# Transposing x and h with VectorE blocks, and applying the graph after the product, in a two-layer graph and attention kernel

## The chip, the cores and the metric

The kernel runs on one core of a Trainium2 chip. The metric is the device time of one launch in microseconds. The kernel before takes 3195.14 us, the median of 3 runs (3194.66 to 3195.42).

TensorE, VectorE, ScalarE and GpSimd appear in the profile as PE (weight loads as PEld), DVE, ACT and POOL; SP is the queue from which all DMAs of this kernel are issued.

## The reference, cut to what matters

There are 64 batches (x is 64 x 256 x 512, float32) and one graph `adj` of 256 x 256 with entries 0 and 1. Layer 0 mixes neighbours, layer 1 is attention with 8 heads under the graph as a mask. Both add their input and normalise.

```python
# layer 0
mi = x @ Wi.T                      # 256 x 512 per batch
mj = x @ Wj.T
deg = a.sum(axis=1)
out = deg[:, None] * (mi + b) + a @ mj
h = layernorm(x + out)
# layer 1
q, k, v = h @ Wq.T + bq, h @ Wk.T + bk, h @ Wv.T + bv
attn = softmax(where(adj == 0, -inf, q k^T / 8))
h2 = layernorm(h + (attn v) @ Wo.T + bo)
```

The graph can be applied before the product or after it: a @ (x @ Wj.T) is the same number as (a @ x) @ Wj.T. On this choice the change turns.

## The kernel before

The batches are worked in 32 pairs (`g`, with batches `b1` and `b2`). While the attention of pair g runs, layer 0 of pair g+1 is done in between, as work items dropped into the attention's slots. All products of layer 0, and the q, k, v and output projections, are done by a seven-product scheme for a 2 x 2 block matrix product (seven block products in place of eight), with sums of the left blocks S1 to S4 and of the right blocks T1 to T4. Everything is float32, except the graph product, where x is split into a rounded part `xhi` and a remainder `xlo` (both float32r) that are multiplied separately by the exactly representable graph.

Layer 0 before: TensorE computes, for each batch, degree times x and neighbour sums of x, already transposed (feature on the partitions), from x as the stationary operand. These are the left blocks of the seven products.

```python
def graph_product(b, c, pa, n, t, part):          # 16 of these for a batch, 384 columns each
    matmul(pa[:, t * P:(t + 3) * P], part[:, t, c * P:(c + 1) * P], graph[:, t, :], ...)

def take_input(b, c, pa):                         # 4 of these for a batch
    nc.scalar.copy(xl[b][:, c]..., pa[:, :3 * P])
    _, a12, a22, a21 = (pa[:, m * P:(m + 1) * P] for m in range(4))
    nc.vector.tensor_add(f["S1"][:, c], a21, f["A22"][:, c])      # 128 x 128 each
    nc.vector.tensor_sub(f["S3"][:, c], f["A11"][:, c], a21)
    nc.vector.tensor_sub(f["S2"][:, c], a22, f["S3"][:, c])
    nc.vector.tensor_sub(f["S4"][:, c], a12, f["S2"][:, c])

def l0_steps(b, norm=norm):
    def product(name, lname, n, first):           # 7 steps, 4 matmuls of 256 columns each
        for c in range(NC):
            matmul(banks[name], xS[b][lname][:, c, :], w0[:, n, c, :], ...)
    ...
    def step7():
        product("z", "S4", B22, False)
        add_to(place(0, 1), banks["z"])
        norm(xh[b][:, 0, :])

def h_transpose(b, t, borrow=False):              # 2 for a batch: h is needed with features on partitions
    for c in range(NC):
        transpose(pt[:, c, :], xh[b][:, t, c * P:(c + 1) * P], ident)      # TensorE, 128 x 128
    nc.scalar.copy(hT[g][:, :, i * N + t * P:i * N + (t + 1) * P], pt)

def split_x(b):                                   # for each batch
    round_x(b)                 # xhi, ScalarE
    remainder(b, nc.gpsimd)    # xlo, GpSimd
    add_bias(b)                # xh += degree * bias, GpSimd
```

The products go to a ring of 3 PSUM banks (`bank`), the scores to a ring of 2 slots of 2 banks (`score_banks`), the attention values to one bank. The weights of the four projections are streamed from device memory, 8 blocks ahead (`bring`, `next_factor`).

The slots of one pair: `work[0]` to `work[6]` hold layer 0 of the next pair.

```python
return [[item(l0_inputs, b1, 0, ...), item(l0_inputs, b1, 1)],
        p[0:3] + [item(split_x, b2)] + p[3:4],
        p[4:7] + [item(l0_inputs, b2, 0)],
        [item(l0_inputs, b2, 1, ...), q[0], q[1], item(h_transpose, b1, 1, True),
         q[2], item(h_transpose, b1, 0, True)],
        q[3:],
        [item(h_transpose, b2, 1, True)], [item(h_transpose, b2, 0, True)]]
```

Of the kernel before, what the change touches and what calls it, by code (L numbers as in the profile page):

```python
# [16 lines left out]
P = 128  # L17
# [203 lines left out]
RIGHT = (B11, T4, B21, T2, T1, T3, B22)  # L221
RIGHT_O = (B11, B21, T4, T2, T1, T3, B22)
# [3 lines left out]
def unshifted_path(ctx, tc, flag, x, adj, wiT, wjT, b0, wqT, bq, wkT, bk, wvT, bv, woT, bo, out):  # L226

# [16 lines left out]
    DH = 64  # L244
    NB = 2
# [47 lines left out]
    adj_i = p2.tile([P, NT, N], I32, tag="pe", name="adj_i")  # L293
    nc.sync.dma_start(out=adj_i, in_=adj.rearrange("(t p) j -> p t j", p=P))
# [6 lines left out]

    load_x(0)
    b_bc = p4.tile([P, D], F32, tag="u", name="b_bc")
    w0 = const.tile([P, 7, NC, H], F32, name="w0")

    for n, w, j in ((B11, wiT, 0), (T3, wiT, 1), (B22, wjT, 1), (B21, wjT, 0)):
        nc.sync.dma_start(out=w0[:, n], in_=w.rearrange("(c p) o -> p c o", p=P)[:, :, j * H:(j + 1) * H])
    nc.sync.dma_start(out=b_bc, in_=b0.to_broadcast([P, D]))
    load_x(1)

    xhi, xlo, xl, xS, hT, hS, qT, kT, vv, aoT, oS = ({} for _ in range(11))

    def round_x(b):

        xhi[b] = p1.tile([P, NT, D], F32R, tag="xhi", name="xhi")
        in_order(nc.scalar.copy(xhi[b], xh[b]))

    round_x(0)


# [12 lines left out]

    graph = const.tile([P, NT, 3 * P], F32R, name="graph")
# [3 lines left out]
    nc.vector.tensor_copy(a, adj_i)  # L338
    aT = p3.tile([P, NT, N], F32, tag="pk", name="aT")
    deg = small.tile([P, NT], F32, tag="deg", name="deg")  # L340
    nc.vector.tensor_reduce(deg, a, AX.X, ALU.add)

    def diagonal(t):
        return slice(2 * t * P, (2 * t + 1) * P)

    def edges(t):
        return slice((1 - t) * P, (3 - t) * P)

    for t in range(NT):
        nc.vector.tensor_scalar(graph[:, t, diagonal(t)], ident, deg[:, t:t + 1], None, ALU.mult)  # L350
    for t in range(NT):
        pt = bank("pt_a")[:, :N]
        for i in range(NT):
            transpose(pt[:, i * P:(i + 1) * P], a[:, i, t * P:(t + 1) * P], ident)

        nc.vector.tensor_copy(graph[:, t, edges(t)], pt)
        in_order(nc.scalar.copy(aT[:, t, :], pt))
# [3 lines left out]
    def check_graph():  # L361


        exact = p1.tile([P, NT, 3 * P], F32, tag="oS", name="exact")
        for t in range(NT):
            in_order(nc.vector.tensor_copy(exact[:, t, edges(t)], aT[:, t, :]))
            in_order(nc.vector.tensor_scalar(exact[:, t, diagonal(t)], ident, deg[:, t:t + 1], None, ALU.mult))
        in_order(nc.vector.tensor_tensor(exact, exact, graph.bitcast(F32), ALU.not_equal))
        in_order(nc.vector.tensor_reduce(inexact, exact.rearrange("p t n -> p (t n)"), AX.X, ALU.max))
        in_order(nc.vector.tensor_scalar(maskT, aT, 0.0, MASK, ALU.is_equal, ALU.mult))  # L370
# [5 lines left out]
    def remainder(b, engine):  # L376

        xlo[b] = p1.tile([P, NT, D], F32R, tag="xlo", name="xlo")
        in_order(engine.tensor_tensor(xlo[b], xh[b], xhi[b].bitcast(F32), ALU.subtract))

    def add_bias(b):
        in_order(nc.gpsimd.tensor_tensor(xh[b], xh[b], degb, ALU.add))

    def split_x(b):
        if b < B:
            round_x(b)
            remainder(b, nc.gpsimd)
            add_bias(b)
# [21 lines left out]
    def blocks_of(w):  # L410
        return w.rearrange("(h c p) (j o) -> p h c j o", h=2, p=P, j=2)

    sources = {}

    def load_raw(w, tag):
        raw = p1.tile([P, 2, 2, 2, H], F32, tag=tag, name="raw")
        nc.sync.dma_start(out=raw.rearrange("p h c j o -> p (h c) (j o)"),
                          in_=w.rearrange("(c p) o -> p c o", p=P))
        return raw

    def make_factors(w, name, raw):
# [3 lines left out]
        for n, (t, p, m) in enumerate(((t1, b12, b11), (t2, b22, t1), (t3, b22, b12), (t4, b21, t2))):  # L425
            in_order(nc.vector.tensor_sub(t, p, m))
            nc.sync.dma_start(out=kept[n], in_=t)
        src = blocks_of(w)
        sources[name] = {B11: src[:, 0, :, 0], B21: src[:, 1, :, 0], B22: src[:, 1, :, 1],
                         T1: kept[0], T2: kept[1], T3: kept[2], T4: kept[3]}  # L430

    def fold_value_bias(raw):

        pb = bank("pb")
        spread = p3.tile([P, NC, P], F32, tag="pk", name="spread")
        in_order(nc.vector.tensor_copy(spread, bv_t.unsqueeze(2).to_broadcast([P, NC, P])))
        for c in range(NC):
            h, kc = divmod(c, 2)
            matmul(pb, spread[:, c], raw[:, h, kc].rearrange("p j o -> p (j o)"),
                   start=(c == 0), stop=(c == NC - 1))  # L440
        nc.vector.tensor_add(bo_bc, pb, bo_bc)
# [49 lines left out]
    def input_tiles(b):  # L491
        xl[b] = p2.tile([P, NC, 3, P], F32, tag="xl", name="xl")
        a11, a12, a22 = (xl[b][:, :, m, :] for m in range(3))
        xS[b] = left_blocks(a11, a12, None, a22, p2.tile([P, 4, NC, P], F32, tag="xS", name="xS"))

    def graph_product(b, c, pa, n, t, part):
        matmul(pa[:, t * P:(t + 3) * P], part[:, t, c * P:(c + 1) * P], graph[:, t, :],
               start=(n == 0), stop=(n == 2 * NT - 1), skip_group_check=True)

    def take_input(b, c, pa):  # L500
        nc.scalar.copy(xl[b][:, c].rearrange("p m n -> p (m n)"), pa[:, :3 * P])
        _, a12, a22, a21 = (pa[:, m * P:(m + 1) * P] for m in range(4))
        f = xS[b]
        nc.vector.tensor_add(f["S1"][:, c], a21, f["A22"][:, c])
        nc.vector.tensor_sub(f["S3"][:, c], f["A11"][:, c], a21)
        nc.vector.tensor_sub(f["S2"][:, c], a22, f["S3"][:, c])
        nc.vector.tensor_sub(f["S4"][:, c], a12, f["S2"][:, c])

    def l0_inputs(b, half, borrow=()):


        if half == 0:
            input_tiles(b)
        for c in (2 * half, 2 * half + 1):
            pa = borrow[c % 2]("pa") if borrow else bank("pa")
            for n, (t, part) in enumerate((t, part) for t in range(NT) for part in (xhi[b], xlo[b])):
                graph_product(b, c, pa, n, t, part)
            take_input(b, c, pa)

    def first_inputs(b):  # L520

        input_tiles(b)
        pas = [score_banks("pa")[:, 0, :], score_banks("pa")[:, 0, :],
               ps_v.tile([P, 2, N], F32, tag="av", name="pa").rearrange("p r q -> p (r q)"), bank("pa")]
        f = xS[b]
        for k, part in enumerate((xhi[b], xlo[b])):
            for c in reversed(range(NC)):
                for t in range(NT):
                    graph_product(b, c, pas[c], k * NT + t, t, part)
                if k == 1:  # L530
                    in_order(nc.scalar.copy(xl[b][:, c].rearrange("p m n -> p (m n)"), pas[c][:, :3 * P]))  # L531

        def add(name, c, x, y, sign):
            in_order(nc.vector.tensor_tensor(f[name][:, c], x, y, ALU.add if sign > 0 else ALU.subtract))  # L534

        def sums(name):
            for c in reversed(range(NC)):
                _, a12, a22, a21 = (pas[c][:, m * P:(m + 1) * P] for m in range(4))
                if name == "S2":
                    add("S3", c, f["A11"][:, c], a21, -1)  # L540
                    add("S2", c, a22, f["S3"][:, c], -1)
                elif name == "S1":
                    add("S1", c, a21, f["A22"][:, c], 1)
                else:
                    add("S4", c, a12, f["S2"][:, c], -1)

        return sums

    def l0_steps(b, norm=norm):
        banks = {}  # L550

        def product(name, lname, n, first):
            if first:
                banks[name] = bank("po")[:, :H]
            for c in range(NC):
                matmul(banks[name], xS[b][lname][:, c, :], w0[:, n, c, :], start=(first and c == 0),
                                 stop=(c == NC - 1), skip_group_check=True)

        def place(t, j):
            return xh[b][:, t, j * H:(j + 1) * H]  # L560

        def add_to(dst, src, order=anywhere):
            order(nc.vector.tensor_add(dst, src, dst))  # L563

        def step1():
            product("x", "A11", B11, True)
            u1 = p2.tile([P, H], F32, tag="lu", name="u1")
            nc.scalar.copy(u1, banks["x"])

            rest = xh[b].rearrange("p t (j o) -> p (t j) o", j=2)[:, 1:]  # L570
            nc.gpsimd.tensor_tensor(rest, rest, u1.unsqueeze(1).to_broadcast([P, 3, H]), ALU.add)  # L571

        def step2():
# [515 lines left out]
```

## Time and profile before

| engine | busy us | share of the span | instructions |
|---|---|---|---|
| PE | 3172.0 | 99% | 17398 |
| PEld | 2621.1 | 82% | 17398 |
| DVE | 1845.7 | 58% | 3848 |
| POOL | 1501.8 | 47% | 1190 |
| ACT | 1109.4 | 35% | 2146 |

The DMA queues move 340.88 MB, at a mean of 107 GB/s. How to read it: "busy" is the time in which an engine had at least one instruction under way. A matmul's record runs from its start to its modelled end, and matmuls overlap, so the mean duration of one record is longer than what it costs in a stream; the cost in a stream is read from the timeline, as the distance of one start to the next. A float32 matmul leaves two records, a float32r matmul and a transpose one.

### The profile page before, as it was taken

The numbers are of one execution on the slowest core, as the hardware profiler recorded it, in microseconds if no ns is written. First come the engines' busy times: TensorE is split into PE (matmuls) and PEld (weight loads), VectorE is DVE, ScalarE is ACT, GpSimd is POOL, SyncE is SP. The second block draws the span as 40 slices with busy tenths as digits, with TensorE's granted clock in tenths as the row PEclk, the third lists the DMA queues.
The fourth block names the chain that finished last, engine by engine and source line by source line (L and its number), as shares of the span: only waits on it lengthen the run. The fifth ranks groups of instructions, "written<-read, shape, count | busy, mean of one in ns | idle before, by whom it ended". The sixth has DMA issues, their size and how long they took to land. (4 is left out here: it accounts for less than half of the span.)

```text
span 3195.0 us, 48126 instructions
## 1 busy us (share of the span) xinstructions
PE 3172.0 (99%) x17398; PEld 2621.1 (82%) x17398; DVE 1845.7 (58%) x3848; ACT 1109.4 (35%) x2146; POOL 1501.8 (47%) x1190
## 2 busy tenths in 40 slices
PE   8999999999999999999999999999999999999998
PEld 6888888888888888888888888888888888888885
DVE  7555556555565555665556555556555565555664
ACT  2333333343333333333333333333343333333333
POOL 2454444544445544445444454444544445544443
PEclk9999999999999999999999999999999999999999
DMA  7234432344322444323443233432344322344222
GB/s 254 68 104 119 123 112 67 96 121 124 119 72 88 116 122 123 86 79 108 126 122 95 75 106 119 124 111 67 96 121 124 116 74 88 116 122 122 82 68 92
DMA packets 257166, 340.88 MB, mean 107 GB/s; under 512 B 29856, under 2 KB 154272, under 8 KB 256928
## 3 DMA queue, kind: packets, MB, share of 16 engines
q1 hardware_dynamic: 256928, 337.76, 35.6%
q8 instruction: 142, 2.33, 0.3%
q14 instruction: 96, 0.79, 0.1%
HBM read 274.73 MB, written 37.75 MB: 98 GB/s over the span
## 5 line engine op out<-in xcount | busy, mean ns | idle before, releaser
L469 POOL TENSOR_TENSOR rstd<-ve,mhalf 128x1 f32<-128x1 f32 x256 | 140.4, 553 | 790.4 <-DVE below L467 790.4
L287 PE MATMUL po<-w,xS 128*128 128x256 f32 x2048 | 466.3, 381 | 2.5 <-DVE xS L534 2.5
L287 PE MATMUL st<-hS,factor 128*128 128x256 f32 x2048 | 454.4, 380 | 2.0 <-DVE u L670 2.0
L797 POOL TENSOR_TENSOR pk<-pe 128x512 f32<-128x512 f32 x256 | 322.8, 1276 | 276.4 <-ACT pe L794 276.4
L287 PEld LDWEIGHTS po<-w,xS 128*128 128x128 f32 x2048 | 386.3, 190 | 64.7 <-DVE rden L867 10.3
L287 PEld LDWEIGHTS st<-hS,factor 128*128 128x128 f32 x2048 | 390.2, 191 | 55.7 <-DVE u L670 2.4
L794 ACT ACTIVATE pe<-pe 128x1024 f32<-128x1024 f32 x256 | 270.2, 1057 | 248.8 <-DVE pe L790 248.8
L287 PE MATMUL po<-w,xl 128*128 128x256 f32 x1536 | 351.0, 381 | 1.5 <-ACT xl L531 0.7
L287 PE MATMUL st<-hT,factor 128*128 128x256 f32 x1536 | 342.2, 379 | 1.0 <-DVE qT L701 1.0
L670 DVE TENSOR_TENSOR u<-st,u 128x512 f32<-128x512 f32 x96 | 66.4, 692 | 468.6 <-PE st L287 461.8
L790 DVE TENSOR_TENSOR pe<-ps,maskT 128x1024 f32<-128x1024 f32 x256 | 297.1, 1201 | 67.6 <-PE ps L287 67.6
L563 DVE TENSOR_TENSOR xh<-po,xh 128x256 f32<-128x256 f32 (+1 forms) x384 | 172.4, 463 | 276.2 <-POOL xh L571 197.9
L287 PEld LDWEIGHTS st<-hT,factor 128*128 128x128 f32 x1536 | 291.7, 190 | 40.9 <-DVE qT L701 1.4
L287 PEld LDWEIGHTS po<-w,xl 128*128 128x128 f32 x1536 | 286.1, 190 | 47.6 <-issue 10.3
L287 PE MATMUL ps<-qT,kT 64*128 64x256 f32 x2048 | 256.5, 389 | 0.0
L287 PE MATMUL pav<-pe,v_sb 128*64 128x256 f32 x2048 | 250.1, 386 | 1.9 <-ACT pe L794 1.8
L287 PEld LDWEIGHTS ps<-qT,kT 64*128 64x128 f32 x2048 | 187.0, 186 | 68.2 <-issue 51.3
L287 PE MATMUL st<-factor,hS 128*128 128x256 f32 x1024 | 234.8, 382 | 0.0
L287 PE MATMUL st<-factor,oS 128*128 128x256 f32 x992 | 229.4, 379 | 0.0
L725 DVE TENSOR_TENSOR xh<-st,xh 128x512 f32<-128x512 f32 x186 | 144.9, 779 | 135.9 <-PE st L287 135.9
L867 DVE RECIPROCAL rden<-den 128x256 f32<-128x256 f32 x96 | 168.8, 1758 | 92.8 <-PE den L287 86.3
L474 ACT ACTIVATE shift<-below,rstd 128x1 f32<-128x1 f32 x256 | 74.9, 293 | 421.3 <-POOL rstd L469 416.4
(117 smaller groups left out, 5032.4 us busy)
## 6 DMA issues: line engine op xcount, KB each, us to landing
xh<-in_x_dram SPq DMA_DIRECT2D x64, 512.0 KB, 4.0
factor<-wq SPq DMA_DIRECT2D x128, 256.0 KB, 2.7
factor<-wk SPq DMA_DIRECT2D x128, 256.0 KB, 2.6
factor<-wv SPq DMA_DIRECT2D x128, 256.0 KB, 4.4
factor<-wo SPq DMA_DIRECT2D x124, 256.0 KB, 2.8
out_dram<-xh SPq DMA_DIRECT2D x62, 512.0 KB, 4.3
factor<-in_wqT_dram SPq DMA_DIRECT2D x96, 256.0 KB, 2.8
factor<-in_wkT_dram SPq DMA_DIRECT2D x96, 256.0 KB, 2.8
```

What stands on the lines that cost most here:

```text
L287: in_order(nc.tensor.matmul(*args, **kw))
L469: nc.gpsimd.tensor_tensor(rstd, ve, mhalf, ALU.pow)
L474: order(nc.scalar.activation(shift, below, AF.Identity, scale=rstd))
L563: order(nc.vector.tensor_add(dst, src, dst))
L670: nc.vector.tensor_add(new("u2"), bank["y"], k["u1"])
L725: nc.vector.tensor_add(dst, src, dst)
L790: nc.vector.tensor_add(pe.rearrange("p j t q -> p j (t q)"), ps.rearrange("p j t q -> p j (t q)"), maskT.rearrange("p t q -> p (t q)").uns ...
L794: in_order(nc.scalar.activation(flat, flat, AF.Exp, scale=QSCALE, accum_out=etot[:, NB * g + i, pr:pr + 1]))
L797: nc.gpsimd.tensor_tensor(pk, pe[:, :, 0, :], pe[:, :, 1, :], ALU.add)
L867: nc.vector.reciprocal(rden, den)
```

## The change: what it does and what it is for

Layer 0 multiplies x itself, not its neighbour sums: mi and mj come from one seven-product scheme over x (row halves, feature halves) and the weights [Wi, Wj] side by side. Then mj is split into a rounded part `hi` and a remainder `lo`, and TensorE applies the graph to them; degree times mi is added by VectorE as it takes mi out of PSUM. For that, x is needed transposed. The transposes are taken off TensorE: x is loaded a second time in a rearranged form (`xB`), in which VectorE's transpose of 32 x 32 blocks gives the transposed matrix (with features in another order, to which the weights' rows are matched). h is transposed in the same manner: it is written to device memory (`h_cols`), read back rearranged (`hB`), and turned by VectorE. Only the first pair still uses TensorE's transposes. The start of the kernel and the order of the work items are rewritten for this.

The diff, cut to its core (removed setup code, renamed tiles and the start of the kernel are left out where marked):

```diff
-RIGHT = (B11, T4, B21, T2, T1, T3, B22)
+RIGHT = (B11, B21, T4, T2, T1, T3, B22)
...
+    def load_xB(b):
+            xB[b] = p1.tile([P, N // R, P], F32, tag="xB", name="xB")
+            for q in range(D // P):
+                nc.sync.dma_start(out=xB[b][q * R:(q + 1) * R],
+                                  in_=x[b][:, q * P:(q + 1) * P].rearrange("(r a) n -> r a n", r=R))
...
-        matmul(pa[:, t * P:(t + 3) * P], part[:, t, c * P:(c + 1) * P], graph[:, t, :], ...)
...
+    def transposed(dst, blocks):
+        in_order(nc.vector.transpose(dst.rearrange("p c (n a) -> p a c n", n=R),
+                                     blocks.rearrange("p a (r c) -> p a c r", c=NC)))
+
+    def turn_x(b, tag="xT"):
+            xT[b] = p1.tile([P, NC, N], F32, tag=tag, name="xT")
+            transposed(xT[b], xB.pop(b))
+            load_xB(b + 1)
+
+    def sum_x(b):
+            a11, a12, a21, a22 = (xT[b][:, 2 * k:2 * k + 2, t * P:(t + 1) * P] ...)
+            xS[b] = left_blocks(a11, a12, a21, a22, p1.tile([P, 4, 2, P], F32, tag="xS", name="xS"))
+            for step in left_steps(xS[b], in_order):        # 4 sums of 128 x 256
+                step()
...
-            for c in range(NC):
-                matmul(banks[name], xS[b][lname][:, c, :], w0[:, n, c, :], ...)      # 256 columns
+            for c in range(2):
+                matmul(banks[name], left[:, c, :], w0[:, n, c, :], ...)              # 512 columns
...
+        def add_scaled(t, src):                   # three for a batch
+            nc.vector.scalar_tensor_tensor(xh[b][:, t, :], src, deg[:, t:t + 1], xh[b][:, t, :],
+                                           ALU.mult, ALU.add)
+        def split(t):
+            nc.scalar.copy(k["hi"][:, t, :], k["mj"][:, t, :])
+            nc.gpsimd.tensor_tensor(k["lo"][:, t, :], k["mj"][:, t, :], k["hi"][:, t, :].bitcast(F32),
+                                    ALU.subtract)
...
         def step7():
-            add_to(place(0, 1), banks["z"])
-            norm(xh[b][:, 0, :])
+            product("z", xS[b]["S4"], B22, False)
+            nc.vector.tensor_add(k["mj"][:, 0, :], banks["z"], k["u2"])
+            split(0)
+
+        def neighbours():                         # 8 matmuls of 512 columns
+            k["pa"] = score_banks("pa")
+            for i in (1, 0):
+                for n, (j, part) in enumerate((j, part) for j in (1, 0) for part in ("hi", "lo")):
+                    matmul(k["pa"][:, i, :], graph[:, j, i * P:(i + 1) * P], k[part][:, j, :], ...)
+
+        def take(t):
+            in_order(nc.vector.tensor_add(r, k["pa"][:, t, :], r))
+            stats[t] = norm_stats(r, in_order)
+        def give(t):
+            norm_apply(xh[b][:, t, :], *stats[t], in_order)
...
+    def send_h(b, t):
+        nc.sync.dma_start(out=h_cols[b][:, t * P:(t + 1) * P, :].rearrange("q p n -> p q n"),
+                          in_=xh[b][:, t, :].rearrange("p (q n) -> p q n", n=P))
+        if t == 0:
+            hB[b] = p1.tile([P, N // R, P], F32, tag="hB", name="hB")
+            nc.sync.dma_start(out=hB[b].rearrange("p a n -> p (a n)"),
+                              in_=h_cols[b].rearrange("q (r a) n -> (q r) (a n)", r=R))
+    def turn_h(b):
+        transposed(hT[g][:, :, i * N:(i + 1) * N], hB.pop(b))
+        if i == NB - 1:
+            sum_h(g)
...
+        return [p[:3] + [item(turn_x, b2)] + p[3:4],
+                p[4:7] + [item(sum_x, b2), item(add_bias, b2)] + q[:1],
+                p[7:10], p[10:] + q[1:3],
+                q[3:6] + [item(turn_h, b1)] + q[6:7],
+                q[7:], [item(turn_h, b2)]]
...
+        neighbours, take1, take0, give1, send1, give0, send0 = work[SLOTS + 1]
+        inverses = divide_at_once(g, w + 1, lambda: run([o[0], neighbours, take1, take0]))
+        run([q[0], give1, send1, o[1], give0, send0, *left_steps(oS[g], in_order), k[0], q[1], k[1]])
...
+        run(o[2:6] + work[SLOTS + 2] + [v[0], o[6], v[1]])
```

Here `p` and `q` inside `layer0` are the step lists of the two batches (7 products, then neighbours, take, give and send); `q`, `k`, `v`, `o` in the last lines are the product steps of the projections.

## The prediction

> **What bounds the kernel now.** I began with the page's busy times and slices, then cut off the start and the end with the table by windows, and only then went to TensorE's timeline for what things cost in a stream. The windows' columns are: stretch, length, then the busy time (and records) of PE, PEld, DVE, ACT and POOL, the granted clock, the DMA share and GB/s.
>
> ```profile
> PE 3172.0 (99%) x17398; PEld 2621.1 (82%) x17398; DVE 1845.7 (58%) x3848; ACT 1109.4 (35%) x2146; POOL 1501.8 (47%) x1190
> ...
> 100.00:3100.00 3000.00, 3000.00 (x16558) 2488.82 (x16558) 1728.02 (x3617) 1052.93 (x2038) 1437.48 (x1132) 1.00 0.35 103
> ```
>
> Between 100 and 3100 us TensorE has no gap at all, at full clock; the table of waits for that stretch is empty for PE. So only TensorE's own work can be saved, and every new wait of TensorE costs its full length. The next view is TensorE's timeline (start, length, operation, shape, records):
>
> ```profile
> 1505.59 3.62 PE L287 MATMUL po<-w,xl 128*128 128x256 f32 x16
> 1509.05 0.60 PE L290 MATMUL pt_h<-ident,xh 128*128 128x128 f32 x4
> 1509.48 1.89 PE L287 MATMUL po<-w,xl 128*128 128x256 f32 x8
> ...
> 1572.65 0.53 PE L287 MATMUL pa<-graph,xhi 128*128 128x384 f32 x1
> 1573.02 0.33 PE L287 MATMUL pa<-graph,xlo 128*128 128x384 f32 x1
> 1573.19 0.34 PE L287 MATMUL pa<-graph,xhi 128*128 128x384 f32 x1
> ...
> 1575.49 0.34 PE L287 MATMUL pa<-graph,xlo 128*128 128x384 f32 x1
> 1575.76 1.95 PE L287 MATMUL pav<-pe,v_sb 128*64 128x256 f32 x16
> ...
> 1671.35 0.53 PE L287 MATMUL pa<-graph,xhi 128*128 128x384 f32 x1
> ```
>
> Read the starts, not the lengths. The sixteen float32 records from 1505.59 to 1509.05 take 3.46 us, 0.216 us each, though their mean duration in the groups is 381 ns. Four transposes take 0.43 us. Sixteen graph matmuls take 1572.65 to 1575.76, 3.11 us, 0.176 us each after the first. This matters: the groups list 189.1 + 171.7 us for the graph product, or 5.6 us a batch, because hi and lo alternate and each record overlaps the next; the stream shows a bit over half of that. The same point comes again at 1671.35: one pair of batches takes 98.70 us. The second batch's graph product is in two pieces, 1.51 us (from 1504.08) and 1.69 us (from 1596.71), 3.20 us.
>
> [...] I estimate 1.22 us for one turn of 1024 columns; no trace here shows one yet. [...]
>
> **The change part by part, on TensorE.**
> - Seven products: 28 matmuls of 256 columns become 14 of 512. Before, 56 records x 0.216 = 12.1 us a batch. The only 512-wide float32 stream of the trace is the last output projection, 24 records from 3176.18 to 3186.58, 0.433 us each, twice 0.216. So 28 x 0.433 = 12.1 us. Nothing gained.
> - Graph product: 16 of 384 columns become 8 of 512. [...] The first and last of a series cost about 0.27 us extra (check on before: 16 x 0.176 + 0.27 = 3.09, read 3.11). So 2.10 us a batch; a pair goes from 3.11 + 3.20 = 6.31 to 4.20 and saves 2.11 us.
> - Transposes of h: four series a pair at 0.43, 1.73 us a pair, gone in all but the first pair. Transposes of x add none, as VectorE makes them.
>
> A pair: 98.70 - 2.11 - 1.73 = 94.86 us. Over the kernel: 32 x 2.11 + 31 x 1.73 = 121 us. The time without a new wait is 3195 - 121 = 3074 us.
>
> **On the other engines**, beside TensorE as long as it isn't made to wait:
> - VectorE loses the small sums (four groups of 252, 283.5 us) and the old additions to xh (128.5 + 44.0 us). It gains four sums of 256 columns a batch ([...] 0.42 us: 64 x 4 x 0.42 = 108), eight operations of 512 columns a batch at 0.69 us (three scaled adds, u2, u3, one mj, two takes: 64 x 8 x 0.69 = 353) and 126 turns at 1.22 us (154). Net 108 + 353 + 154 - 456 = +159 us: about 2005 us, 65% of the new span.
> - ScalarE loses 117.0 (xl), 66.6 (xhi), 62 of 64 parts of 74.9 (hT) and 22.8 us (u), and gains four copies a batch at 586 ns, 150 us. Net about -129.
> - GpSimd loses 148.5 (xlo) and 117.2 us (L571) and gains three operations a batch of 512 columns at 1.28 us, 246 us. Net about -20.
> - DMA gains x a second time, and h out and back: (64 + 62 + 62) x 0.524 MB = 98.5 MB on 341. At 3080 us that is 143 GB/s. The start of the kernel, at 311 GB/s in the first 20 us, shows that there is room.
>
> **The rivals.**
> 1. *The new round trip of h becomes TensorE's wait.* Counted from the end of a batch's graph product: two takes with statistics on VectorE (2 x (0.69 + 0.69 + 0.47) = 3.7 us), 0.55 us for the power on GpSimd, 2 x (0.29 + 0.81) us on ScalarE, then the store (256 KB, a factor block of that size lands in 2.7 us) and the load (512 KB, 4.0 us like x), then the turn 1.2 us: some 14.5 us, and more with queues. For b2 TensorE has in the meantime six steps of 1.73 us (q, o, k, q, k, o) and three more (o), 15.6 us, then three further steps (v, o, v) before the first product that needs this h, about 20.8 us in all. It fits with 6 us to spare. For b1 it is closer. VectorE works in order, and the turn stands ahead of the addition that makes mj of b2. VectorE reaches it after some 14 us (scores 1.0, two steps 3.4, values, denominators and scores 4.4, three products 5.2), and b2's own chain to its graph product (mj 0.69, copy 0.59, remainder 1.28, against 4.6 us of other products) forgives about 2 us more. With queues on VectorE and GpSimd I count 14 to 17 us against 16. A wait of up to 2 us in many pairs is likely enough; 31 x 2 = 62 us would leave 3136.
> 2. *The remainder `lo` comes late.* mj is made out of step 7's bank, copied by ScalarE, subtracted by GpSimd at 1.28 us, where two more such operations and the attention's sums (1276 ns each) queue. Slack is about 5 us for 2.6 us of chain. A miss would be under 1 us a pair, 30 us.
> 3. *VectorE becomes the bound.* At 65% it isn't on average. If one turn takes 4 us rather than 1.2, VectorE is at 77%, and TensorE waits for banks (three only) where a turn and four sums stand ahead of an eviction: perhaps 1 to 3 us a pair, 3110 to 3170 us.
> 4. *The start.* TensorE idles some 12 us in the first 80 now. The new start has x transposed without TensorE but waits for the weights in an order of its own and loads x twice; I take it as even, plus or minus 8 us.
>
> **Range and chances.** 3074 plus 12 us for new waits (0.4 us a pair, mostly from rival 1) gives 3086 us. The lower end, 3058, is no waits, a better start [...]. The upper end, 3132, has rival 1 in nearly every pair. The 2% line is 3131: I give 0.87 to faster, 0.10 to within 2%, 0.03 to slower, which needs rivals 1 and 3 together.
>
> **What the changed kernel's profile would show.** TensorE still at 98 to 99%, the distance between the same points of two pairs near 95 us; eight `pa` records of 512 columns about 0.23 us apart and pt_h in the first pair only; VectorE's turns near 1.2 us; VectorE near 2000 us, POOL near 1480, ACT near 980, DMA near 439 MB. If rival 1 holds, the waits of PE list `pa` released by the remainder on GpSimd, or `st` released by hS or hT on VectorE, some 31 times, and VectorE waits for the DMA into hB. I am wrong if [...] a turn takes several us, or if the round trip takes over 20 us.

## The result, and the profile after

The changed kernel takes 3117.14 us, the median of 4 runs (3115.85 to 3117.91), against 3195.28 us before: a ratio of 0.9755 (95% interval 0.9738 to 0.9772), or 78 us less. The prediction was 3086 us, 109 us less. The direction and the two savings that it rests on were right; 31 us of the expected gain did not come.

The page's first part for the changed kernel:

```profile
PE 3082.4 (99%) x14598; PEld 2131.7 (68%) x14598; DVE 2227.6 (71%) x3327; ACT 998.4 (32%) x1894; POOL 1504.5 (48%) x1255
```

And the same stretch as before from the table by windows, with its columns as before:

```profile
100.00:3100.00 3000.00, 2992.44 (x14291) 2074.76 (x14290) 2154.00 (x3206) 971.51 (x1844) 1470.03 (x1222) 1.00 0.46 138
```

TensorE is still the bound, but it is no longer without gaps: 7.6 us of the 3000 are idle, where there were none. VectorE has 382 us more than before, where I expected 159.

TensorE's timeline around the two graph products of a pair, and the same point one pair later:

```profile
1532.07 2.00 PE L290 MATMUL ps<-qT,kT 64*128 64x256 f32 x16
...
1552.77 1.98 PE L290 MATMUL po<-w,xS 128*128 128x512 f32 x4 [0.18 <-ACT mj L547]
1554.59 1.88 PE L290 MATMUL po<-w,xT 128*128 128x512 f32 x4
...
1558.85 1.13 PE L290 MATMUL ps<-qT,kT 64*128 64x256 f32 x8
1559.91 0.50 PE L290 MATMUL pa<-hi,graph 128*128 128x512 f32 x1
1560.25 0.40 PE L290 MATMUL pa<-lo,graph 128*128 128x512 f32 x1
1560.48 0.40 PE L290 MATMUL pa<-hi,graph 128*128 128x512 f32 x1
...
1561.66 0.39 PE L290 MATMUL pa<-lo,graph 128*128 128x512 f32 x1
1561.98 1.13 PE L290 MATMUL ps<-qT,kT 64*128 64x256 f32 x8
...
1628.08 2.00 PE L290 MATMUL ps<-qT,kT 64*128 64x256 f32 x16
```

A pair now takes 1628.08 - 1532.07 = 96.01 us (95.99 is the median of the 31 distances; only the first is far off it, 97.50), not the 94.86 of the prediction. The graph product costs 1559.91 to 1561.98, 2.07 us, 0.235 us a matmul. The prediction's 2.10 us a batch was the author's estimate, as no trace before shows this matmul at 512 columns; the 0.176 us that it takes there at 384 columns, times 512 / 384, gives the same 0.235. The wait in brackets is small, but it stands in every pair. The table of TensorE's waits says so (us in total, times, longest):

```profile
PE po L290 <- DVE xT L485: 10.9, 2, 8.2
PE po L290 <- ACT mj L547: 5.7, 31, 0.2
```

The first line is the start; the second comes 31 times. These idle times understate what a wait costs. From start to start, the record before this wait takes 0.35 us and the first one after it 0.10 us more than the 0.43 of their neighbours: 0.45 us, not 0.18. To see where the rest went I summed the distances from each TensorE record to the next over a pair (medians of the pairs of each trace):

| TensorE's stream in one pair, us | before | after | difference | predicted |
|---|---|---|---|---|
| graph product | 6.31 | 4.12 | -2.19 | -2.11 |
| transposes of h | 1.84 | 0 | -1.84 | -1.73 |
| seven products of layer 0 | 24.29 | 25.17 | +0.88 | 0 |
| projections (q, k, v, o) | 48.47 | 48.70 | +0.23 | 0 |
| scores | 7.71 | 7.91 | +0.20 | 0 |
| values and denominators | 10.08 | 10.08 | 0 | 0 |
| the pair | 98.69 | 95.99 | -2.70 | -3.84 |

The two savings came in full. Three rows that the prediction held unchanged took 1.3 us back. Over 31 pairs the saving is 84 us, not 119. The rest is mostly the start: the whole kernel saved 79.2 us of profiled span (3195.0 to 3115.8), so what lies outside the pairs, with the 1.5 us by which the first pair is longer, got 4.5 us longer, where the prediction had 2 us shorter.

VectorE's groups (busy, mean ns | idle before) show the size that I had wrong:

```profile
L485 DVE STREAM_TRANSPOSE xT<-xB 128x1024 f32<-128x1024 f32 x64 | 134.3, 2098 | 6.0 <-DMA xB<-in_x_dram 6.0
L485 DVE STREAM_TRANSPOSE hT<-hB 128x1024 f32<-128x1024 f32 x62 | 132.5, 2138 | 0.0
...
L479 DVE TENSOR_TENSOR xS<-xT 128x256 f32<-128x256 f32 x64 | 60.2, 941 | 0.0
L480 DVE TENSOR_TENSOR xS<-xT,xS 128x256 f32<-128x256 f32 x64 | 60.1, 939 | 0.0
```

A turn takes 2.1 us, not 1.22, and two of the four small sums 0.94 us, not the 0.42 that VectorE's addition of 128x256 takes in the trace before (418 ns). But the second line's idle time of 0.0 says that VectorE never waited for h's round trip.

### The profile page after: what moved, and what is told of

The parts are those of the page before. It is cut to its first block, busy times and chain, and to the rows that moved or that the text cites. A ratio compares the mean times of both kernels' runs of the same rounds, so it can differ in the third digit from the quotient of the medians.

```text
span 3115.8 us, 42525 instructions
## 1 busy us (share of the span) xinstructions
PE 3082.4 (99%) x14598; PEld 2131.7 (68%) x14598; DVE 2227.6 (71%) x3327; ACT 998.4 (32%) x1894; POOL 1504.5 (48%) x1255
## 2 busy tenths in 40 slices
DMA packets 398490, 439.13 MB, mean 141 GB/s; under 512 B 36928, under 2 KB 288320, under 8 KB 397888
## 5 line engine op out<-in xcount | busy, mean ns | idle before, releaser
L290 PE MATMUL po<-w,xS 128*128 128x512 f32 x1024 | 471.7, 603 | 6.1 <-ACT mj L547 5.7
L290 PE MATMUL po<-w,xT 128*128 128x512 f32 x768 | 354.0, 603 | 12.9 <-DVE xT L485 10.9
L290 PEld LDWEIGHTS po<-w,xS 128*128 128x128 f32 x1024 | 187.5, 190 | 253.5 <-issue 192.6
L290 PE MATMUL st<-hT,factor 128*128 128x256 f32 x1536 | 360.1, 381 | 0.7 <-ACT hT L622 0.7
L290 PEld LDWEIGHTS po<-w,xT 128*128 128x128 f32 x768 | 144.1, 191 | 181.0 <-issue 163.3
L290 PE MATMUL ps<-qT,kT 64*128 64x256 f32 x2048 | 264.9, 392 | 0.0
L290 PEld LDWEIGHTS pav<-pe,v_sb 128*64 128x64 f32 x2048 | 135.2, 136 | 154.2 <-issue 71.9
L888 POOL TENSOR_TENSOR rtot<-rtot,rden 128x256 f32<-128x256 f32 x96 | 70.0, 729 | 332.2 <-DVE rden L887 332.2
L290 PEld LDWEIGHTS st<-factor,hS 128*128 128x128 f32 x1024 | 191.9, 190 | 35.4 <-issue 10.6
```

Of the source, the lines that this page charges most:

```text
L290: in_order(nc.tensor.matmul(*args, **kw))
L888: nc.gpsimd.tensor_tensor(rtot, rtot, rden, ALU.add)
```

## The experiments

The theory after the comparison: TensorE lost in each pair 0.45 us at the seventh product, which waits for ScalarE to copy mj out of its bank; 0.27 us in the projections, where a bank of k waits for ScalarE; and the rest at changes between the half-array products of the attention (64*128 and 128*64 in the profile's lines) and full ones (128*128), with the start on top. The rival: VectorE, 71% busy and with turns of twice the expected length, is in the way everywhere, and the waits that show are only where it comes out.

### The mj copy earlier

```diff
-        return [p[:3] + [item(turn_x, b2)] + p[3:4],
-                p[4:7] + [item(sum_x, b2), item(add_bias, b2)] + q[:1],
+        return [p[:3] + [item(turn_x, b2)] + p[3:5],
+                p[5:7] + [item(sum_x, b2), item(add_bias, b2)] + q[:1],
```

> The fifth product of the first batch of each pair moves one slot earlier, ahead of the scores. Theory A: in every pair TensorE loses 0.45 us in the seventh product because ScalarE copies mj out of its bank only after two exponentials that stand ahead in its queue; the copy is then early, the wait goes in all 31 pairs, about -14 us, so near 3103 us, and no wait of TensorE for the mj copy is left. Theory B: that wait is only the last of several that end at about the same time (the fourth product's bank is then emptied behind the 2.1 us turn of x on VectorE): the wait moves to another place, 0 to +10 us.

Measured: 3117.53 us (3117.37 to 3120.2), nothing gained. The pair's table shows why: the seven products lose their 0.45 us (25.17 to 24.72), and the graph product grows by 0.51 (4.12 to 4.63). TensorE's waits of this kernel:

```profile
PE pa L290 <- POOL lo L525: 7.2, 31, 0.2
```

The copy was the cause of the wait at that place, but not of the pair's length. With the product gone from between the scores and the graph product, the graph product came 1.7 us sooner after those scores and met the remainder on GpSimd, the prediction's rival 2. Theory B was right in its outcome, with the wait at another place than it named.

### The k product before the second half of h's normalisation

```diff
-        run([q[0], give1, send1, o[1], give0, send0, *left_steps(oS[g], in_order), k[0], q[1], k[1]])
+        run([q[0], give1, send1, o[1], k[0], give0, send0, *left_steps(oS[g], in_order), q[1], k[1]])
```

(on top of the edit above)

> As mj_early, and the first k product of the next pair is put ahead of the second half of h's normalisation in ScalarE's queue. Theory A: the third product of k waits 0.27 us in each pair for ScalarE to empty a bank, behind the normalisation; this goes too, -8 us more, near 3095 us in all. Theory B: h of the second batch is then sent 0.84 us later and its round trip, which I held to be close to its limit, shows as a wait of TensorE: the 8 us are lost or more.

Measured: 3109.93 us (3109.27 to 3110.42), 7.6 us less than with the first edit alone, as theory A had it. The weight loads of the projections show the wait going (columns as above); first the changed kernel, then this one:

```profile
L290 PEld LDWEIGHTS st<-hT,factor 128*128 128x128 f32 x1536 | 289.0, 190 | 52.4 <-ACT u L711 11.8 <-ACT hT L622 0.9 <-issue 0.5
```

```profile
L290 PEld LDWEIGHTS st<-hT,factor 128*128 128x128 f32 x1536 | 291.5, 190 | 42.3 <-ACT hT L622 0.9 <-issue 0.5
```

The release by ScalarE's eviction (L711) is gone. It stood behind two normalisations of h at 0.81 us in ScalarE's queue. The PE wait table did not list this at all; it was seen only in the weight loads and in the starts.

### h turned by TensorE again

```diff
     def send_h(b, t):
-        ...                       # the store of h and the rearranged load
+        pass
     def turn_h(b):
-        ...                       # VectorE's turn
+        h_transpose(b, 1, True)
+        h_transpose(b, 0, True)
```

> Only the turning of h goes back to TensorE (eight transposes and two ScalarE copies a batch); the store, the load and VectorE's turn of h are left out. Theory A: the round trip of h is wholly hidden, so what it saved is the stream time of the transposes, 1.84 us a pair: +57 us, near 3174 us. Theory B: VectorE at 71% already holds TensorE back in places, and gets 132 us of turns off its hands here: less than +40 us.

Measured: 3171.16 us (3169.16 to 3172.29), 54.0 us more than the changed kernel, near theory A's 57. This divides the change: turning h on VectorE brings 54 of the 78 us, close to the prediction's 31 x 1.73 = 53.6 us. The new layer 0, with its start, brings the other 24 us (3195.3 to 3171.2), where the prediction had 32 x 2.11 = 67.5 from the graph product. So in sum the missing gain belongs to layer 0. The close agreement for h is in part luck: the transposes cost 1.91 us a pair here, not 1.73, and the pair grew by only 1.68, since the 0.24 us in the projections, a cost of turning h on VectorE, went away too.

### Every turn made twice

```diff
+        if again:
+            transposed(dst, blocks, False)
```

(at the end of the function that makes a turn)

> Every turn of x and h is made twice, 126 more at 2.1 us on VectorE, 267 us more work for it (71% to about 79% busy). Theory A: VectorE's turns lie beside TensorE's work with slack of a few us each; TensorE loses at most 0.5 us a pair, 0 to +15 us. Theory B: VectorE is the second bound and in the way where products wait for their banks: 1 us for each turn or more, +60 to +150 us.

Measured: 3190.25 us (3188.38 to 3191.87), 73 us more, 0.58 us for each extra turn of 2.1. Theory A's limit of 15 us falls. VectorE is at 78%. TensorE's waits:

```profile
PE po L290 <- ACT mj L549: 36.2, 31, 1.2
...
PE st L290 <- ACT u L713: 14.8, 31, 0.5
PE st L290 <- PE st L290: 9.8, 31, 0.3
```

The mj wait grows from 0.18 to 1.17 us, the eviction by ScalarE (L711 above, L713 here) now shows in TensorE's own table at 0.5, and a third place is new. The first two are named after ScalarE, but VectorE was slowed. All engines of the changed kernel in the stretch before the mj copy show the chain behind them:

```profile
1547.10 1.76 DVE L887 RECIPROCAL rden<-den 128x256 f32<-128x256 f32 x1 [0.89 <-PE den L290]
1548.77 2.29 DVE L805 TENSOR_TENSOR pe<-ps,maskT 128x1024 f32<-128x1024 f32 x2
...
1549.96 1.06 ACT L809 ACTIVATE pe<-pe 128x1024 f32<-128x1024 f32 x1 [2.87 <-DVE pe L805]
...
1551.10 1.06 ACT L809 ACTIVATE pe<-pe 128x1024 f32<-128x1024 f32 x1
...
1552.15 0.57 ACT L547 COPY mj<-po 128x512 f32<-128x512 f32 x1
```

Denominators, reciprocal (1.76 us, VectorE), two score sums (2.29 us, VectorE), two exponentials (2.1 us, ScalarE), then mj's copy, then TensorE's seventh product. In brackets at the first line: VectorE had 0.89 us to spare there. One more turn of 2.1 us takes up the 0.89 and passes 1.2 on; the wait grew by 1.0. So by this reading the long turn did not cause the mj wait in the changed kernel, but the spare time was 0.9 us, not several.

### The turn in plain order

```diff
-        in_order(nc.vector.transpose(dst.rearrange("p c (n a) -> p a c n", n=R),
-                                     blocks.rearrange("p a (r c) -> p a c r", c=NC)))
+        in_order(nc.vector.transpose(dst,
+                                     blocks.rearrange("p (c b) n -> p c (b n)", c=NC)))
```

The second form keeps the writing side's stride and has only the reading side plain: `blocks.rearrange("p a (c r) -> p a c r", c=NC)`. Both put the elements in an order that the weights don't match, so their outputs are not the reference's; only times are read from them.

> The turn of VectorE reads and writes its 1024 columns in plain order, without the strides of 4 and 8 elements; the feature order is then not the one that the weights have, so the output is another one. Only the times are compared. Theory A: [...] whatever the strides: 2.1 us again, and the time stays within 3 us of the changed kernel. Theory B: the strides cost it: 1.2 us a turn, VectorE 110 us less busy, and TensorE gets part of it back, 0 to -15 us.

> The changed kernel with only the reading side of the turn in plain order; the writing side keeps its stride of 8 elements. The features come in another order than the weights have, so the output is another one; only times are compared. In plain order on both sides a turn took 1.24 us, with both strides 2.10 us. If the read stride of 4 elements (16 bytes) is the cost: 1.24 us and near 3110 us; if the write stride of 8 elements (32 bytes) is: 2.10 us and near 3117 us; if both share in it, in between.

Measured: 3110.05 us (3107.8 to 3110.71) with both sides plain, 3113.8 us (3112.79 to 3114.05) with the reading side plain. VectorE's groups of the first and of the second:

```profile
L485 DVE STREAM_TRANSPOSE xT<-xB 128x1024 f32<-128x1024 f32 x64 | 79.1, 1235 | 6.4 <-DMA xB<-in_x_dram 6.4
```

```profile
L485 DVE STREAM_TRANSPOSE xT<-xB 128x1024 f32<-128x1024 f32 x64 | 130.9, 2046 | 6.5 <-DMA xB<-in_x_dram 6.5
```

The plain turn takes 1.24 us, what the prediction estimated; the write stride of 8 elements costs 0.8 us of the 2.1. That is theory B. The extra time of 126 turns is 111 us on VectorE and 7 us on TensorE. It sits in the projections: st from hT falls from 10.60 to 10.36 us a pair, the wait that the k product's move took away as well. The mj wait stays (5.7 us, 31 times), as the reading of the chain has it. So of the missing gain the rival named at the head of these experiments explains 7 us: turns that are 111 us shorter in all are worth no more. The gain does not follow the length of the turn either: with only the reading side plain a turn is 0.05 us shorter (2.05 for 2.10), and 3.3 us are gained, 0.14 us a pair, all of it in the projections.

### The first graph product later

```diff
-                p[7:10], p[10:] + q[1:3],
+                [], q[1:3] + p[7:],
```

> Only the first batch's graph product moves: behind the second scores and two products, not between the two scores. Theory A: each change of TensorE from the half-array products of the scores to full ones costs it 0.3 to 0.4 us; one such change less a pair is -10 to -12 us, near 3105 us. Theory B: the round trip of h, which starts 4.5 us later, had about 2 us to spare at VectorE's turn; VectorE then waits for the load of h about 2 us in each pair and what stands behind the turn comes late: +15 to +50 us.

Measured: 3145.79 us (3143.96 to 3146.59), 28.6 us more, as theory B had it. The scores lose their 0.20 us (7.71 a pair again), but VectorE's waits now have:

```profile
DVE hT L485 <- DMA hB<-h_cols: 78.0, 31, 3.8
```

2.5 us a pair, where the changed kernel had none. The round trip that rival 1 feared had about 2 us to spare and no more: in the changed kernel's pair shown above the load of h landed at 1575.53 and the turn started at 1577.90. The scores' 0.20 us is so shown to come from splitting them. The rest of the price of a change between half-array and full products can't be read from this run, because the waits cover it.

### The product put back, and GpSimd's bias

```diff
-                p[4:7] + [item(sum_x, b2), item(add_bias, b2)] + q[:1],
-                p[7:10], p[10:] + q[1:3],
+                p[5:7] + [item(sum_x, b2), item(add_bias, b2)] + q[:2],
+                p[7:10], p[10:] + q[2:3],
```

(with p[4] in the list before, and with the k product's move; the later form has `item(add_bias, b2)` behind `item(turn_x, b2)`)

> As both_orders, and one product of the second batch is put in the place that the fifth product left, so that as much of TensorE's work as in the changed kernel stands between the scores and the first batch's graph product. Theory A: the run with the early mj gained nothing because the graph product then came 1.7 us sooner and waited for the remainder on GpSimd [...]; with the work put back between them both waits go: 14 us below both_orders, near 3096 us, and neither the mj copy nor the remainder is in TensorE's table of waits. Theory B: VectorE's queue (reciprocal, score sums, turn) sets the pace of this stretch whatever the order: the wait turns up at a third place and the time stays within 3 us of both_orders.

Measured (this run is called balanced): 3263.05 us (3260.92 to 3263.33), 153 us more than without the move, and slower than the kernel before (ratio 1.0207, 1.0193 to 1.0221). TensorE's and VectorE's waits:

```profile
PE ps L290 <- DVE pe L805: 98.8, 31, 3.2
```

```profile
DVE xh L520 <- POOL xh L374: 148.5, 32, 4.7
```

VectorE, in order, met the scaled addition of the second batch before GpSimd had added the bias to the same tile, and stood there 4.7 us a pair. The score sums behind it came late, and TensorE waited 3.2 us a pair for a bank of scores. My theory of this run had not looked at that order at all. The wait is not the whole loss. TensorE's records behind it in one pair:

```profile
1635.85 2.08 PE L290 MATMUL ps<-qT,kT 64*128 64x256 f32 x8 [3.18 <-DVE pe L805]
1637.86 3.78 PE L290 MATMUL po<-w,xT 128*128 128x512 f32 x4
```

The changed kernel's timeline above has 1.13 and 1.88 us for the same two. For some 5 us behind the wait TensorE works at half rate in this pair, with full-width records 0.85 us apart and not 0.43. Scores and layer 0 together grow by 2.0 us a pair, of the 4.9 that a pair grew, and the mean granted clock of this run is 0.976 (0.999 in the changed kernel).

> As balanced, and GpSimd adds the degree bias to the second batch one slot earlier. Theory A: balanced lost 153 us only because VectorE, which works in order, reached the scaled addition of the second batch before GpSimd had added the bias (4.7 us a pair), so that the scores' banks came free late (3.2 us a pair for TensorE); with the bias early this wait goes, and what balanced was to show is seen: both the mj and the remainder waits gone, 14 us below both_orders, near 3096 us. Theory B: VectorE's queue sets the pace of this stretch whatever the order: 3105 us or more, with a wait at another place.

Measured (called balanced_bias): 3139.52 us (3138.77 to 3141.22). The mj wait and the remainder wait are both gone, as meant, and a third has come, at the attention's values:

```profile
PE pav L290 <- ACT pe L809: 29.5, 33, 1.0
```

The product taken from behind the second scores had covered the exponentials there. So theory B holds for the orders tried: moving a product each time opened another wait. None of the orders of these products that were tried was better than the changed kernel's own.

### The start, and the best version

> As balanced, and x of the first two batches is loaded once and turned by TensorE. Theory A: the changed kernel's start loses some 4 us before TensorE's first product (the rearranged load lands at 6.0 us, the turn takes 2.1) and 2.8 us at the second batch, whose rearranged load comes late: both go, 4 to 7 us less than balanced, near 3091 us. Theory B: the start is held by the loads of the weights, the bytes arrive no sooner: within 2 us of balanced.

> As balanced_bias, and the start with TensorE's transposes of the first two x, which took 5 us off balanced. By theory A 5 us below balanced_bias, near 3091 us; by theory B the 5 us may be the only gain over both_orders, near 3105 us.

```diff
-    load_xB(0)
+    load_x(0)
...
-    turn_x(0)
+    pe_turn_x(0)       # 8 transposes by TensorE, 2 copies by ScalarE; the same for batch 1
```

Measured: 3257.98 us (3256.72 to 3258.91) on top of balanced and 3134.93 us (3134.27 to 3136.95) on top of balanced_bias: 5.1 and 4.6 us less, the 4 to 7 of the first run's theory A. The start is a cost of the new layer 0, and TensorE's transposes take part of it back.

> The changed kernel with only the two edits that gained: the first k product ahead of the second half of h's normalisation, and TensorE's transposes of the first two x. If the two gains are independent, 7.6 + 5 us off 3117: near 3104.5 us, with a pair near 95.73 us (0.24 to 0.27 us less) and the rest at the start. If the start only moves a wait of the first pair to another place, near 3109 us.

Measured: 3104.42 us (3104.14 to 3104.8), a ratio of 0.9715 (0.9702 to 0.9729) to the kernel before, 12.7 us less than the changed kernel: the two gains add. TensorE's first records of this kernel:

```profile
5.11 1.95 PE L293 MATMUL pt_x<-ident,xh 128*128 128x128 f32 x8 [5.11 <-DMA xh<-in_x_dram]
6.88 3.78 PE L290 MATMUL po<-w,xT 128*128 128x512 f32 x4
```

The first product starts at 6.88 us, not at 8.15. That is 1.3 us; the changed kernel's first products are also slow:

```profile
8.15 3.78 PE L290 MATMUL po<-w,xT 128*128 128x512 f32 x4 [8.15 <-DVE xT L485]
12.69 3.75 PE L290 MATMUL po<-w,xT 128*128 128x512 f32 x4 [0.76 <-ACT u L530]
...
20.77 1.88 PE L290 MATMUL po<-w,xT 128*128 128x512 f32 x4
```

In its first 32 us nine records of layer 0 stand 0.85 us apart, in the fastest version two. How much of the 5 us comes from this is not shown, since TensorE waits in between. The pair is at 95.75 us. This is the fastest version that was run.

## Why the prediction was right and wrong

- **The bound and the two savings: right.** The graph product was sized at -2.11 us a pair and measured -2.19, the transposes at -1.73 and -1.84. Reading starts and not durations decided this: the groups' durations fall by 360.8 - 212.2 = 149 us, 4.6 us a pair, for the same two kernels, twice what the stream shows. "Nothing gained" for the wider products: right too, 0.429 us a record of 512 columns against 2 x 0.216, which is 0.2 us a pair less.
- **The allowance of 12 us for new waits, "mostly from rival 1": this is the step that failed.** Its size was too small and its cause was another. Rival 1 did not happen: VectorE started its turn of b1 15.9 us after the end of the graph product (1577.90 against 1561.98), where the prediction counted some 14, and the load of h had landed at 13.6 us, 2.4 us before. In that batch the second store landed at 1572.23, the load was issued at 1572.29 and landed at 1575.53: two transfers, one after the other. What came in its place were two waits on ScalarE's queue. One no rival named: 0.45 us a pair at mj, 14 us in all. The run with the mj copy early takes exactly this out of the products, but another wait took its place, so that these 14 us could not be won back by that move. The other is 0.27 us at k, 8 us; the run with the k product's move gained 7.6. It goes away with the plain turn too, so it is rival 3 in small: a turn of 2.1 us holds an eviction back there, one of 1.24 us does not.
- **A term that was left out.** The prediction charged matmuls, not the places where TensorE changes between the half-array products of the attention and full ones. Splitting the scores around the graph product costs 0.20 us a pair in the scores. Three more series of layer 0 now end at such a place, at 0.09 us each; before, the graph product and the transposes ended there, so the prediction took those ends away with them. Together some 0.5 us a pair, 15 us. The 0.20 went away in the run with the later graph product; the 0.09 are read from the trace and not from an experiment.
- **The turn at 1.22 us: too small by 0.9 us.** The 1.22 us was the author's estimate: the trace before shows no turn, only VectorE's additions of the same 1024 columns, at 1225 ns. The plain turn comes near it with 1.24 us. What the estimate left out is the write stride, which costs 0.8 us. VectorE came to 2228 us, not 2005: 113 us from turns, 75 us from the small sums, 15 us from the scaled additions; some 20 us are not placed. On TensorE the stride cost 7 us, through the same wait at k.
- **Rival 3: sharper than I put it.** VectorE isn't the bound at 71%, but a doubled turn cost 73 us. I had it as a matter of a mean share; the spare time at the place that counts was 0.9 us.
- **The start, "even, plus or minus 8 us":** 6.6 us worse than the prediction's sum, within what was stated. The rearranged load landed at 6.04 us, the turn took 2.06, and the first product started at 8.15 us; before, TensorE's first work started at 4.11. The half rate of the first products, shown above, was not in the prediction.
- Bytes (439.13 MB), GpSimd (1504.5 us against about 1480) and ScalarE (998.4 against about 980) came near their estimates.

The sum: 35 us short in the pairs and about 6.6 in the rest is 42 us, of which 12 were allowed for, and 30 remain (31 by the median times).

## What to carry to other kernels

When one engine is full, what a change removes from it can be sized from the distances of starts to within some per cent; what it gives back comes from chains through the other engines, so follow each new eviction back through the queue of the engine that makes it, and count the spare time there, not the engine's share. A wait named after one engine (ScalarE here) can be a chain that began three steps earlier on another. Moving work to take a wait away has to be judged by the length of the whole period: of four such moves here one gained, and three opened another wait.

## What the runs showed of the hardware that was not expected

- A VectorE transpose of 1024 float32 columns takes 1.24 us in plain order, 2.05 us with a write stride of 8 elements, and 2.10 us with a read stride of 4 as well. So the writing side's stride costs 0.8 us; plain writing with strided reading was not run.
- VectorE's small sums took longer beside GpSimd's work: in the changed kernel the third one took 1.51 us from 1556.19, while GpSimd's two remainders ran from 1556.09 to 1558.84, and 0.42 us from 1530.95, with no GpSimd instruction under way. In the balanced run, with another order of the work, the same sum has a mean of 0.415 us, and the first two, at 0.52 and 0.46 us in the changed kernel, have 0.75 and 0.92. That GpSimd is the cause is a reading of these traces; no run here isolated it.
- After some waits TensorE worked at half rate for a while. In the run with the product put back, full-width records stood 0.85 us apart, not 0.43, behind a wait of 3.2 us, and in the changed kernel's start after the waits of 8.15 and 2.78 us. It did not follow every wait: not the 31 of 1.2 us in the run with every turn made twice, and not one of 2.48 us at the start of the kernel before.
